# The lists of sources of a graph kernel: 17 gathers of pieces for three nodes each, moved into place on VectorE, for 49 gathers of a list for one node each

## The chip, the core and the metric

The kernel runs on one core of a Trainium2 chip. The time is device microseconds of a whole execution, the median of the runs. One further execution was recorded by the hardware profiler, and all views shown here are of that one. The engines are called by the names of the profile: PE (TensorE matmul) and PEld (its weight loads), DVE (VectorE), ACT (ScalarE), POOL (GpSimd), SP (SyncE, here only a queue of DMAs). "L998" is line 998 of the kernel.

## The reference, cut to what matters

The input is a table `x` of 6250 nodes with 256 features and 100000 edges `src`, `dst`, sorted by `dst`, so that the sources of all edges into one node stand in one run of `src`.

```
x = layernorm(x + two_gatv2_layers(x, edges and a loop at each node))   # 4 heads of 64
x = layernorm(x + gat_layer(x, edges))                                  # 8 heads of 32

xl, xr = x @ Wl, x @ Wr                                  # of each gatv2 layer
logit  = sum over a head of att * leaky_relu(xl[src] + xr[dst])
alpha  = softmax of logit over the edges of one dst
out    = sum over the edges of one dst of alpha * xl[src]  + b
```

## The kernel before, in words

The kernel has two parts, one after the other: `make_plan`, and `tile_by_degree`, which runs the three layers. A third part, `tile_general_path`, runs instead of the layers if the plan finds that its assumptions do not hold (the flag `fits`).

**The layers.** The nodes are put in order of their degree and taken 128 at a time, in NB = 49 blocks. In one block each partition holds one node, and all nodes have about the same number of edges. For each block POOL issues one indirect DMA for each rank of edge (`gather_rows`, L1235): 128 rows of the table, one to a partition. What a node needs for that, the list of its sources (CM = 38 numbers, filled up with the number of an empty row) and its row of `x`, lies in the DRAM table `near_d`, one row to a node in the order of their numbers, and is fetched by `start1` (L1595) with an indirect DMA by `node_i`, the node at each place of the order. The first three fetches come ahead of all gathers of the first layer.

**The plan.** `make_plan` has to deliver four things: `node_i`; the lists in `near_d`; the first layer's table `xl1_d` (x times a weight matrix, 49 blocks of 128 rows, `tables(n)` does the next n blocks); and the place of each node in the order, written beside its row of that table (`place_f`, L1058, 4 bytes to a row). It runs by an order written out by hand; each engine takes its instructions in that order, and so does the queue of each engine that issues DMAs.

1. DVE finds the ends of the runs in `dst` (`ends`, `part`), makes one-hot matrices `oh_lo`, `oh_hi` of the node's two digits, and PE adds up `count`, a [128, 49] table of degrees. A node n is at partition n mod 128 and column n div 128.
2. From `count` come the places at which the lists begin (`begin_i`): PE adds whole columns and the partitions above, DVE sums them up.
3. POOL gathers, for each of the 49 columns, 38 numbers of `list_d` (a copy of `src` in DRAM) from `begin_i` on: one indirect DMA for 128 nodes, 152 bytes each (L998), into `near`.
4. Meanwhile DVE and PE find the order of degrees: one-hot keys `oh`, running sums `cum` by matmuls `pk` in blocks of 512 (`cuts`), `place_f`, the one-hot `to_hi`, `given`, `to_lo`, and the matmuls `pp` that give `node_i`.
5. `lacking` marks which of the 38 numbers are beyond a node's degree, `fill` replaces them (a copy under a mask, L1013) and sends nine columns to `near_d` by a DMA on SP (L1016). The six groups of nine columns (`spans`) are filled where the order by hand puts them: two after step 4, and the others between the tables that are left.
6. DVE adds up what must not be (`wrong`, `bad`), PE sums it over the partitions (`pb`), and `fits` results. `right` and `left` make the weights of the second layer.
7. Between these steps stand `tables(12)`, `(1)`, `(2)`, `(12)`, `(4)`, `(7)` and the remaining 11. One block is: PE turns x (`pt`), ACT copies it (`xT`), PE multiplies (`pm`), ACT copies the row (`xl`, ten buffers), SP sends it to `xl1_d` (L846). SP also loads x (L815) and sends it on to `near_d` (L821), each for seven blocks, and loads the weights `wh` (L1122) and four small rows `fixed` (L1129, L1133) for the later layers.

When the plan ends, its buffers are given to the layers. The first instruction of POOL in the layers (`numbers`, L1182) waits for every DMA and engine that used them.

## Time and profile before

| | us |
|---|---|
| median of 3 runs | 3889.89 (3889.52 to 3891.73) |
| the profiled execution, whole time | 3880.55 |
| its span, first to last instruction | 3878.7 |
| POOL's first gather of lists (L998) begins | 40.07 |
| its last one (of 49) begins | 113.31 |
| last list filled on DVE (L1013) begins | 115.88 |
| POOL's first instruction in the layers (L1182) | 149.98 |
| `start1` of the first block (L1595) | 150.75 |

In the timeline a line is: start, duration, engine, line, operation, output and inputs, how many, and in brackets how long the engine stood idle just before and what ended that. A DMA's instruction on POOL ends when it is issued, not when the data have landed; "SPq" is SP's queue, again the issue. "issue" in brackets is time in which the profile shows nothing that was waited for, and "remote" a release by something it cannot name. Page rows of a group give busy time, mean duration of one in ns, and the idle time before.

### The profile page before, as it was taken

To read this page: it belongs to the slowest core of one execution; us is meant where nothing else is said; L and a number is where in the kernel's file an instruction comes from. 1 tells how busy PE (TensorE), PEld (TensorE's weight loads), DVE (VectorE), ACT (ScalarE), POOL (GpSimd) and SP (SyncE) were. 2 spreads that over 40 slices of the span, in tenths; PEclk is the share of its full clock that TensorE was granted. 3 is DMA by queue.
4 is the path that set the end of the run, shared out by engine and by line. 5 is a ranking of instruction groups with operands and counts; after the bars stand their busy time and mean duration, and the time that the engine had idled before them with its cause. 6 is when DMAs were issued, how large, how long until landed. Compare 5 with 4: busy or idle time off the path is not lost.

```text
span 3878.7 us, 23608 instructions
## 1 busy us (share of the span) xinstructions
PE 1481.8 (38%) x5130; PEld 1113.8 (29%) x5130; DVE 2836.2 (73%) x2648; ACT 1091.1 (28%) x4176; POOL 2530.5 (65%) x2613
## 2 busy tenths in 40 slices
PE   6324665556667763355544545554000000000000
PEld 5213444434555542343433433443000000000000
DVE  6228988668888876899876988896676565666665
ACT  3113444334445442243433434443000000000000
POOL 6464666666666645666666666664777777777774
PEclk8656877778788886676666677776555555555555
DMA  8532333333434334333433434442343333333332
GB/s 188 109 92 78 98 104 104 100 99 103 105 102 108 104 79 109 100 106 104 112 107 105 111 107 110 109 111 74 101 108 101 96 97 96 97 97 96 97 97 57
DMA packets 196123, 395.60 MB, mean 102 GB/s; under 512 B 63036, under 2 KB 115514, under 8 KB 195956
## 3 DMA queue, kind: packets, MB, share of 16 engines
q0 software_dynamic: 122048, 338.04, 33.2%
q1 hardware_dynamic: 66226, 54.22, 5.1%
q10 hardware_dynamic: 7698, 1.74, 0.4%
q8 instruction: 45, 0.74, 0.1%
q14 instruction: 106, 0.87, 0.1%
HBM read 353.82 MB, written 40.42 MB: 102 GB/s over the span
## 4 chain that ended last, share of the span: by engine, by line
issue 20%; POOL 20%; DVE 13%; PE 10%; another core or an unknown queue 6%; ACT 5%; DMA 1%; DVEq 0%; POOLq 0%; ACTq 0%
POOL g L1235 18%; PE acc L1418 6%; DVE z L1505 4%; DVE z L1504 4%; DVE lg L1506 3%; PE pm L1362 3%; ACT g L1410 2%; ACT wt L1381 2%; DVE g L1411 1%; POOL out L1733 1%; DMA g<-xl_d,near_r 1%; DVE weighted L1433 1%; ACT xT L1357 0%; PE pt L1355 0%
## 5 line engine op out<-in xcount | busy, mean ns | idle before, releaser
L1235 POOL DMA_INDIRECT g<-xl_d,near_r x1569 | 1487.4, 948 | 858.7 <-issue 454.3
L1418 PE MATMUL acc<-g,ident 128*128 128x256 f32 x3408 | 1015.9, 461 | 765.3 <-issue 282.7
L1418 PEld LDWEIGHTS acc<-g,ident 128*128 128x128 f32 x3408 | 774.4, 234 | 1004.2 <-issue 522.3
L1235 POOL DMA_INDIRECT g<-whs_d,near_r x766 | 793.2, 1036 | 284.2 <-issue 250.0
L1410 ACT ACTIVATE g<-g,by 128x64 f32<-128x64 f32 x2056 | 545.1, 337 | 316.1 <-issue 310.8
L1504 DVE TENSOR_TENSOR z<-g,pr 128x1820 f32<-128x1820 f32 (+4 forms) x234 | 497.1, 2125 | 19.1 <-DMA g<-xl_d,near_r 10.0
L1505 DVE TENSOR_TENSOR z<-z,at 128x1820 f32<-128x1820 f32 (+4 forms) x234 | 497.4, 2126 | 8.0
L1506 DVE TENSOR_REDUCE lg<-z 128x28 f32<-128x1820 f32 (+4 forms) x234 | 497.3, 2125 | 8.1
L1442 DVE TENSOR_REDUCE acc_v<-weighted 128x256 f32<-128x4096 f32 (+15 forms) x49 | 343.7, 7014 | 16.5 <-remote 8.3
L1411 DVE TENSOR_TENSOR g<-g,wt 128x1792 f32<-128x1792 f32 (+8 forms) x234 | 348.4, 1505 | 2.9
L1391 ACT ACTIVATE wt<-lg 128x128 f32<-128x128 f32 (+17 forms) x49 | 14.0, 285 | 851.0 <-DVE top L1374 391.5
L1703 DVE TENSOR_TENSOR lg<-g,s_r 128x56 f32<-128x56 f32 (+4 forms) x111 | 22.1, 213 | 315.1 <-DMA g<-whs_d,near_r 272.5
L1357 ACT COPY xT<-pt 128x256 f32<-128x256 f32 x147 | 54.9, 374 | 688.5 <-remote 342.2
L1433 DVE TENSOR_TENSOR weighted<-g,wt 128x1792 f32<-128x1792 f32 (+4 forms) x111 | 226.6, 2056 | 0.1
L1571 DVE RECIPROCAL den<-den 128x4 f32<-128x4 f32 x98 | 17.4, 177 | 212.9 <-ACT wt L1381 165.2
L1381 ACT ACTIVATE wt<-lg,top 128x19 f32<-128x19 f32 (+14 forms) x392 | 116.0, 296 | 190.8 <-DVE lg L1506 74.3
L1362 PE MATMUL pm<-wcat,xT 128*128 128x260 f32 x392 | 136.0, 505 | 56.3 <-ACT xT L1357 49.8
L1362 PE MATMUL pm<-wh_cat,xT 128*128 128x272 f32 x196 | 77.5, 531 | 183.8 <-ACT xT L1357 95.5
L1537 DVE TENSOR_TENSOR h<-acc,den 128x256 f32<-128x256 f32 x98 | 40.7, 416 | 126.2 <-remote 112.8
L1362 PEld LDWEIGHTS pm<-wcat,xT 128*128 128x128 f32 x392 | 94.8, 255 | 90.5 <-ACT xT L1357 64.6
L1362 PEld LDWEIGHTS pm<-wh_cat,xT 128*128 128x128 f32 x196 | 42.8, 242 | 203.0 <-ACT xT L1357 104.7
L1362 PE MATMUL pl<-wcat,xT 128*128 128x260 f32 x196 | 64.0, 455 | 55.5 <-issue 40.4
(232 smaller groups left out, 1548.4 us busy)
## 6 DMA issues: line engine op xcount, KB each, us to landing
g<-xl_d,near_r POOLq DMA_INDIRECT x1569
g<-whs_d,near_r POOLq DMA_INDIRECT x766
whs_d<-row SPq DMA_DIRECT2D x49, 132.0 KB
xl_d<-xl SPq DMA_DIRECT2D x49, 130.0 KB
xl_d<-row SPq DMA_DIRECT2D x49, 130.0 KB
xr_d<-row SPq DMA_DIRECT2D x49, 130.0 KB
two<-xl_d SPq DMA_DIRECT2D x49, 130.0 KB
two<-xr_d SPq DMA_DIRECT2D x49, 130.0 KB
```

The costliest lines, as they stand in the source:

```text
L1235: nc.gpsimd.indirect_dma_start(out=g[:, j + own - s0, :width], out_offset=None, in_=table, in_offset=source(of, b, j),)
L1357: nc.scalar.copy(xT, pt)
L1362: nc.tensor.matmul(pm, xT[:, c, :], w[:, c, :], start=c == 0, stop=c == 1)
L1381: nc.scalar.activation(wt[:, :, h], lg[:, :S, h], AF.Exp, bias=top[:, h : h + 1], accum_out=den[:, h : h + 1],)
L1410: nc.scalar.mul(g4[:, t, h, :], g4[:, t, h, :], by[:, t - m, h : h + 1])
L1411: nc.vector.tensor_mul(g4[:, :m], g4[:, :m], wt[:, s0 : s0 + m, :].unsqueeze(3).to_broadcast([P, m, H, F // H]),)
L1418: nc.tensor.matmul(acc, ident, g4[:, t], start=s0 + t == 0, stop=s0 + t == S - 1 and not more)
L1433: nc.vector.tensor_mul(prod[:, s0 - base : s1 - base, :].rearrange("p t (h d) -> p t h d", h=H), g[:, :n, :F].rearrange("p t (h d) -> p t ...
L1442: nc.vector.reduce_sum(part, prod[:, : s1 - base, :].rearrange("p s f -> p f s"), axis=AX.X)
L1504: nc.vector.tensor_max(z, g[:, :n, :W2], xr[:, None, :].to_broadcast([P, n, W2]))
L1505: nc.vector.tensor_mul(z, z, at[:, None, :].to_broadcast([P, n, W2]))
L1506: nc.vector.reduce_sum(lg[:, s0:s1, :], z.rearrange("p t (h d) -> p t h d", h=H2), axis=AX.X)
```

## The change

The number of a node is cut another way: node n is at partition n div 49 and column n mod 49, so that the nodes of one partition are neighbours, and so are their runs in `src`. Division by 49 is a product with `by` and a shift by `down`. One gather now fetches a piece of 133 numbers (532 bytes) for three neighbouring nodes of each partition, from 32 places ahead of the first one's begin; 17 gathers (`SEGS`) cover the 49 columns. `usual` is where each of the three would begin at 16 edges a node; `off` is the deviation from that, cut to 0 to 63 as `off_i`, and its six bits are masks. DVE moves the pieces by powers of two: for each of the three nodes a copy of 69 numbers and a copy under the mask of bit 5 from 32 further on, then for bits 4 to 0 copies under masks within `moved`. A deviation beyond 0 to 63 makes `wrong`.

This stands behind `to_lo` and `pp`, followed by all six `lacking` and `fill`, and only then by `got`, `wrong` and `fits`. The tables are dealt out anew: 12, 1, then one each inside the two loops over `cuts` ahead of the third block and one between the loops, 12, 8 (ahead of `off`), 4, 2 and 7. The four loads of `fixed` come after the last table.

```diff
+    by, down = next(
+        (m, d) for d in range(24, 8, -1) for m in (-(-(1 << d) // NB),)
+        if (NP - 1) * m < 1 << 24 and all(n * m >> d == n // NB for n in range(NP))
+    )
+    assert NP * by >> down >= P
+
+
+    SEGS, STEP, BITS = 17, 3, 6
+    LEAD = 1 << BITS - 1
+    MEAN = E // N
+    LONG = MEAN * (STEP - 1) + CM + 2 * LEAD - 1
+    WIDE = CM + LEAD - 1
+    assert (SEGS - 1) * STEP < NB <= SEGS * STEP
...
-    list_d = dram.tile([-(-E // CM) * CM + CM], I32, name="list_d")
+    list_d = dram.tile([-(-(LEAD + E) // LONG) * LONG + LONG], I32, name="list_d")
...
+    nc.scalar.dma_start(list_d[:LEAD].unsqueeze(0), nothing[:, :LEAD])
+    nc.scalar.dma_start(list_d[LEAD + E :].unsqueeze(0), nothing)
     nc.scalar.dma_start(
-        list_d[:E].rearrange("(a b) -> a b", a=a), src.rearrange("(a b) -> a b", a=a)
+        list_d[LEAD : LEAD + E].rearrange("(a b) -> a b", a=a), src.rearrange("(a b) -> a b", a=a)
     )
...
+    usual = iota("usual", [P, SEGS * STEP], [[0, SEGS], [MEAN, STEP]], base=-LEAD)
...
-    nc.vector.tensor_scalar(
-        part[:, 0, :], run_i, SHIFT, P - 1, op0=OP.logical_shift_right, op1=OP.bitwise_and
+    nc.vector.tensor_single_scalar(part[:, 1, :], run_i, SHIFT, op=OP.logical_shift_right)
+    nc.vector.tensor_single_scalar(part[:, 0, :], part[:, 1, :], float(by), op=OP.mult)
+    nc.vector.tensor_single_scalar(part[:, 0, :], part[:, 0, :], down, op=OP.logical_shift_right)
+    nc.vector.scalar_tensor_tensor(
+        part[:, 1, :], part[:, 0, :], -float(NB), part[:, 1, :], op0=OP.mult, op1=OP.add
     )
-    nc.vector.tensor_single_scalar(part[:, 1, :], run_i, SHIFT + 7, op=OP.logical_shift_right)
...
-    pc = ps.tile([P, 2, NB], F32, name="pc", tag="ph")
-    nc.tensor.matmul(pc[:, 0, :], ones, count, start=True, stop=True)
-    nc.tensor.matmul(pc[:, 1, :], above, count, start=True, stop=True)
+    total = one.tile([P, 1], F32, name="total")
+    nc.vector.reduce_sum(total, count, axis=AX.X)
+    pc = ps.tile([P, 2], F32, name="pc", tag="ph")
+    nc.tensor.matmul(pc[:, 1:], above, total, start=True, stop=True)
+    nc.tensor.matmul(pc[:, :1], ones, total, start=True, stop=True)
+    upto = one.tile([P, NB], F32, name="upto")
+    nc.vector.tensor_tensor_scan(upto, ones_k[:, :NB], count, 0.0, op0=OP.mult, op1=OP.add)
+    within = one.tile([P, SEGS, STEP], F32, name="within")
+    flat = within.rearrange("p s j -> p (s j)")
+    nc.vector.memset(flat[:, NB - 1 :], 0.0)
+    nc.vector.tensor_sub(flat[:, :NB], upto, count)
+    base = one.tile([P, 2], F32, name="base")
+    nc.vector.tensor_copy(base, pc)
+    begin_f = one.tile([P, SEGS], F32, name="begin_f")
+    nc.vector.tensor_scalar(begin_f, within[:, :, 0], base[:, 1:], None, op0=OP.add)
+    begin_i = one.tile([P, SEGS], I32, name="begin_i")
+    nc.vector.tensor_scalar(begin_i, begin_f, float(E), 0.0, op0=OP.min, op1=OP.max)
+    piece_of = one.tile([P, SEGS, LONG], I32, name="piece_of")
+    listed = list_d.rearrange("(a b) -> a b", b=LONG)
+    for k in range(SEGS):
+        nc.gpsimd.indirect_dma_start(
+            out=piece_of[:, k, :], out_offset=None, in_=listed,
+            in_offset=bass.IndirectOffsetOnAxis(ap=begin_i[:, k : k + 1], axis=1),
+        )
     key = one.tile([P, NB], BF16, name="key_b")
     nc.vector.tensor_scalar(key, count, float(high), float(low), op0=OP.min, op1=OP.max)
     nc.vector.tensor_scalar(key, key, -1.0, float(high), op0=OP.mult, op1=OP.add)
...
-    block = one.tile([P, NB], F32, name="block")
-    nc.vector.tensor_copy(block, pc[:, 0, :])
-    upto = one.tile([P, NB], F32, name="upto")
-    nc.vector.tensor_tensor_scan(upto, ones_k[:, :NB], block, 0.0, op0=OP.mult, op1=OP.add)
-    from_f = one.tile([P, NB], F32, name="from_f")
-    nc.vector.tensor_sub(from_f, upto, block)
-    nc.vector.tensor_add(from_f, from_f, pc[:, 1, :])
-    begin_i = one.tile([P, NB], I32, name="begin_i")
-    nc.vector.tensor_scalar(begin_i, from_f, float(E), 0.0, op0=OP.min, op1=OP.max)
-    near = one.tile([P, NB, CM], I32, name="near")
-    no = one.tile([P, NB, CM], I32, name="no")
-    listed = list_d.rearrange("(a b) -> a b", b=CM)
-    for k in range(NB):
-        nc.gpsimd.indirect_dma_start(
-            out=near[:, k, :], out_offset=None, in_=listed,
-            in_offset=bass.IndirectOffsetOnAxis(ap=begin_i[:, k : k + 1], axis=1),
-        )
...
-    spans = [(k, min(NB, k + 9)) for k in range(0, NB, 9)]
-
-    def lacking(k0, k1):
-        shape = [P, k1 - k0, CM]
-        nc.vector.tensor_tensor(
-            no[:, k0:k1, :], ranks[:, None, :].to_broadcast(shape),
-            count[:, k0:k1].unsqueeze(2).to_broadcast(shape), op=OP.is_ge,
-        )
-
-    def fill(k0, k1):
-        shape = [P, k1 - k0, CM]
-        nc.vector.copy_predicated(
-            near[:, k0:k1, :], no[:, k0:k1, :], far[:, None, :].to_broadcast(shape)
-        )
-        nc.sync.dma_start(
-            near_d[k0 * P : k1 * P, :CM].rearrange("(k p) c -> p k c", p=P).bitcast(I32),
-            near[:, k0:k1, :],
-        )
-
-
-    tables(1)
     oh = one.tile([P, KEYS, NB], BF16, name="oh")
     nc.vector.tensor_tensor(
         oh, steps, key[:, None, :].to_broadcast([P, KEYS, NB]), op=OP.is_equal
     )
+
+
+    tables(1)
...
     for c0, c1 in cuts:
+        if c0 == 2 * 512:
+            tables(1)
         pk = ps.tile([P, 512], F32, name="pk", bufs=2)
         nc.tensor.matmul(pk[:, : c1 - c0], ones_b, ohf[:, c0:c1], start=True, stop=True)
         nc.vector.tensor_tensor_scan(
             cum[:, c0:c1], ones_k[:, : c1 - c0], pk[:, : c1 - c0],
             cum[:, c0 - 1 : c0] if c0 else 0.0, op0=OP.mult, op1=OP.add,
         )
-    tables(2)
+    tables(1)
     for c0, c1 in cuts:
+        if c0 == 2 * 512:
+            tables(1)
         pk = ps.tile([P, 512], F32, name="pk", bufs=2)
         nc.tensor.matmul(pk[:, : c1 - c0], less, ohf[:, c0:c1], start=True, stop=True)
         nc.vector.tensor_add(cum[:, c0:c1], cum[:, c0:c1], pk[:, : c1 - c0])
...
-            xl1_d[:NP, W2:].rearrange("(b p) w -> p b w", p=P), place_f.unsqueeze(2)
+            xl1_d[:NP, W2:].rearrange("(p b) w -> p b w", b=NB), place_f.unsqueeze(2)
...
+    tables(8)
+    off = one.tile([P, SEGS, STEP], F32, name="off")
+    nc.vector.tensor_sub(off, within, usual.rearrange("p (s j) -> p s j", s=SEGS))
+    nc.vector.tensor_sub(off, off, within[:, :, :1].to_broadcast([P, SEGS, STEP]))
+    off_i = one.tile([P, SEGS, STEP], I32, name="off_i")
+    nc.vector.tensor_scalar(off_i, off, 0.0, float(2 * LEAD - 1), op0=OP.max, op1=OP.min)
+    bit = one.tile([P, BITS, SEGS, STEP], I32, name="bit")
+    for k in range(BITS):
+        nc.vector.tensor_scalar(
+            bit[:, k], off_i, k, 1, op0=OP.logical_shift_right, op1=OP.bitwise_and
+        )
+    moved = one.tile([P, SEGS, STEP, WIDE], I32, name="moved")
+    for k in range(STEP):
+        for first_at in (0, LEAD):
+            data = piece_of[:, :, MEAN * k + first_at : MEAN * k + first_at + WIDE]
+            if first_at == 0:
+                nc.vector.tensor_copy(moved[:, :, k, :], data)
+            else:
+                nc.vector.copy_predicated(
+                    moved[:, :, k, :],
+                    bit[:, BITS - 1, :, k : k + 1].to_broadcast([P, SEGS, WIDE]), data,
+                )
+    every = moved.rearrange("p s j w -> p (s j) w")
+    bits = bit.rearrange("p b s j -> p b (s j)")
+    for k in range(BITS - 2, -1, -1):
+        n = CM + (1 << k) - 1
+        nc.vector.copy_predicated(
+            every[:, :, :n], bits[:, k, :].unsqueeze(2).to_broadcast([P, SEGS * STEP, n]),
+            every[:, :, 1 << k : (1 << k) + n],
+        )
+    near = every[:, :NB, :CM]
+    no = one.tile([P, NB, CM], I32, name="no")
+    spans = [(k, min(NB, k + 9)) for k in range(0, NB, 9)]
+    def lacking(k0, k1):
+        shape = [P, k1 - k0, CM]
+        nc.vector.tensor_tensor(
+            no[:, k0:k1, :], ranks[:, None, :].to_broadcast(shape),
+            count[:, k0:k1].unsqueeze(2).to_broadcast(shape), op=OP.is_ge,
+        )
+    def fill(k0, k1):
+        shape = [P, k1 - k0, CM]
+        nc.vector.copy_predicated(
+            near[:, k0:k1, :], no[:, k0:k1, :], far[:, None, :].to_broadcast(shape)
+        )
+        nc.sync.dma_start(
+            near_d.rearrange("(p k) c -> p k c", k=NB)[:, k0:k1, :CM].bitcast(I32),
+            near[:, k0:k1, :],
+        )
     for k in spans:
         lacking(*k)
-    fill(*spans[0])
-    fill(*spans[1])
+        fill(*k)
+    tables(4)
     got = one.tile([P, 3, NB], F32, name="got")
     nc.vector.tensor_copy(got, pp)
     nc.vector.scalar_tensor_tensor(
-        node_i, got[:, 1, :], float(P), got[:, 0, :], op0=OP.mult, op1=OP.add
+        node_i, got[:, 0, :], float(NB), got[:, 1, :], op0=OP.mult, op1=OP.add
...
+    nc.vector.tensor_tensor(
+        wrong[:, KE + NB : KE + 2 * NB], off.rearrange("p s j -> p (s j)")[:, :NB],
+        off_i.rearrange("p s j -> p (s j)")[:, :NB], op=OP.not_equal,
+    )
+    nc.vector.tensor_mul(
+        wrong[:, KE + NB : KE + 2 * NB], wrong[:, KE + NB : KE + 2 * NB], count
+    )
     nc.vector.tensor_scalar(
-        wrong[:, KE + NB :], upto[:, NB - 1 :], float(E), None, op0=OP.not_equal
+        wrong[:, KE + 2 * NB :], base[:, :1], float(E), None, op0=OP.not_equal
...
-    tables(4)
+    tables(2)
...
-    fill(*spans[2])
...
-    fill(*spans[3])
...
-    for k in spans[4:]:
-        fill(*k)
```

## Prediction, made before the changed kernel ran

> **What bounds the kernel now.** I read the page first, then the stretch before the layers in the timeline, engine by engine, then its busy time by windows and its waits. The page's rows:
>
> ```profile
> PE 1481.8 (38%) x5130; PEld 1113.8 (29%) x5130; DVE 2836.2 (73%) x2648; ACT 1091.1 (28%) x4176; POOL 2530.5 (65%) x2613
> ...
> L1235 POOL DMA_INDIRECT g<-xl_d,near_r x1569 | 1487.4, 948 | 858.7 <-issue 454.3
> ```
>
> No engine is full. Once the layers run, POOL issues row gathers most of the time, one each 1.25 us (0.95 and 0.30 of issue). The diff leaves these layers alone; it changes what comes ahead of their first gather. The chain of waits starts at 972 us here, so the head has to be read from the timeline. POOL's, cut:
>
> ```profile
> 40.07 1.36 POOL L998 DMA_INDIRECT near<-list_d,begin_i  x1 [17.38 <-DVE begin_i L993]
> ...
> 56.21 2.46 POOL L998 DMA_INDIRECT near<-list_d,begin_i  x1 [0.30 <-issue]
> ...
> 64.12 6.29 POOL L998 DMA_INDIRECT near<-list_d,begin_i  x1 [0.30 <-issue]
> 70.72 0.97 POOL L998 DMA_INDIRECT near<-list_d,begin_i  x1 [0.30 <-issue]
> ...
> 113.31 0.94 POOL L998 DMA_INDIRECT near<-list_d,begin_i  x1 [0.30 <-issue]
> 149.98 0.24 POOL L1182 IOTA numbers<- 128x128 f32 x1 [35.72 <-DMA near_d<-near]
> ```
>
> The 49 gathers of source lists take POOL from 40.07 to 114.25. Then it stands for 35.7 us, until the last list has landed in `near_d`; start1 follows at 150.75 and the layers run from there. The end of that wait is what this change can move, and nothing works beside it: in the windows view DVE is empty from 120 to 150 us.
>
> ```profile
> 82.00:120.00 38.00, 11.63 (x31) 7.79 (x30) 7.14 (x29) 6.75 (x30) 24.64 (x26) 0.52 0.62 101
> 120.00:150.00 30.00, 15.28 (x80) 12.62 (x78) 0.00 (x0) 8.97 (x28) 0.02 (x1) 0.78 0.88 160
> ```
>
> (columns: PE, PEld, DVE, ACT, POOL busy; clock; DMA share; GB/s). Why the lists are that late is on the SP queue and behind it:
>
> ```profile
> 81.57 0.58 DVE L1013 COPY_PREDICATED near<-no,far 128x342 int32<-128x342 int32 x1 [9.16 <-DMA near<-list_d,begin_i]
> ...
> 115.88 0.33 DVE L1013 COPY_PREDICATED near<-no,far 128x152 int32<-128x152 int32 x1 [4.16 <-DMA near<-list_d,begin_i]
> ```
> ```profile
> 141.91 1.35 SPq L1016 DMA_DIRECT2D near_d<-near  x2
> ```
> ```profile
> 110.33 0.38 ACT L845 COPY xl<-pm 128x260 f32<-128x260 f32 x1 [10.14 <-remote]
> 116.61 0.37 ACT L836 COPY xT<-pt 128x256 f32<-128x256 f32 x1 [5.91 <-remote]
> ```
>
> The last list is filled on DVE at 116, but SP issues it at 142.9, behind the rows of the last tables. Those are late because PE and ACT nearly stood from 91 to 117 (PE's clock 0.52), in waits that the trace cannot name; from 119 a table takes 1.1 us again. So two things hold the start: the gathers to 116, and a tail of tables and row writes.
>
> **The change part by part.** Order on the queues, by the diff.
>
> *Before the gathers.* Two more TENSOR_SCALARs on `part` (0.11 apart): +0.25. The ones matmuls become single-column, `block` and two adds give way to total, within, base, begin_f: about even, and the keys now come after begin_i. Gathers start near 40. The first-pass and second-pass loops each get a table ahead of their third block: one table at the low clock is about 1.5 us on DVE's chain (a table was 2.1 us at 42 to 46). So to_hi starts near 54.5 instead of 52.4 and to_lo ends near 71.5 instead of 69.6.
>
> *17 gathers for 49.* 128 rows each as before, so about 0.94 + 0.30: the first ends at 41.4, and by 54.5 some 12 are issued. The rest meet to_hi, three given and to_lo. In the trace one gather ends 0.8 to 0.9 us after each of these (6.29 us at 64.12 under to_lo, 62.91 to 69.59). Five gathers, five instructions: the last ends at 71.5 + 0.9 = 72.4. The Trainium skill, "SBUF — State Buffer", "SBUF: two separate sides", says that a DVE operation with two SBUF inputs takes the shared port from a GpSimd operation that reads SBUF, and a gather reads its indices there. The trace grants that for the bf16 rows above and not in general: `cum`*`oh` (two SBUF inputs, 1.28 us from 48.12) left the gather at 49.23 at 0.99, and `no` left the one at 70.72 at 0.97. By the rule in full, up to three more of the first 12 gathers slip behind the bf16 rows, and POOL ends 3 x 1.25 = 3.8 us later; I take the rows, zero, and keep 3.8 for the range.
>
> *Landing.* place_f's 6272 writes of 4 bytes (L1058, issued 66.16; the new order of rows leaves their number) fill the DMA engines in about 70 to 81. In the trace the second list, whose last gather ended at 74.43, could be filled only at 81.57: 7 us. Idle, 2 us are usual (113.31 + 0.94 to 115.88: 1.6). So the pieces land between 74.5 and 79.5. I take 78, as it is the same storm. Off and the six bits, nine operations of 49 to 51 elements (about 0.2 each, 1.5 us), lie in that wait.
>
> *The moves, all on DVE in series.* The copy with mask has two rows: 342 elements 0.545, 152 elements 0.331; so 0.16 + 1.126 ns an element.
> - three first copies under mask of 17 x 69 = 1173: 1.48 each, 4.4
> - five under mask of 51 x (53, 45, 41, 39, 38) = 11016 elements: 12.4 + 5 x 0.16 = 13.2
> - three plain copies of 1173: the nearest 1-element row gives 1.48 each, 4.4 in all. The Trainium skill, "VectorE: DVE Perf Modes", "What auto-detection actually checks", has a one-source copy in SBUF run two elements a cycle if the outermost dimensions are equal (17 and 17); the TENSOR_SCALAR row (256 elements, 0.276) shows that speed here, and gives 0.75 each, 2.25. I take 2.25; the other end costs 2.2 us.
> Sum 19.9, with hand-overs 20.5. No row has a mask broadcast along its run and a source shifted in its own tile, so the masked price is open: not below the full-rate 1.04 ns (-1.3 us); above, see the rival.
>
> *Then* six lacking and fill pairs: 5 x (0.41 + 0.545) + 0.53 = 5.3, with gaps 5.9 (the L1006 part ran at 69.5 before, beside waiting gathers). Ends 78 + 20.5 + 5.9 = 104.4, with the last near_d issue close behind: 38 us earlier than 142.9. Their landing (six times 1152 rows of 152 bytes) lies beside what follows.
>
> *What stands behind DVE now.* got, node_i, wrong, bad: 2.8 as from 82.04, plus two small ones: 107.6; pb, many, fits 1.6: 109.2. Formerly fits came at 88.4, so the whole tail behind it is 21 us later than it was. On PE, pb stands ahead of the last 7 tables (turned blocks are ready); on ACT left(1) does. left(1): prods at 110.2, eight accumulations of 0.25, ends 112.4. 7 tables: 1.1 each, two of them at 2.1 with the clock down: 10, so 122.4. These 7 were not bounded by fits before but by the standstill, 91 to 122.
>
> *SP.* Rows 37 on wait behind the six near_d issues in queue order; xl has ten buffers, so 28 to 42 go through on PE and ACT with rows up to 36 already issued. Past 104.4 SP has 13 rows at 0.4, two near_d<-xt, two wh loads; this fits before 122.8. The four fixed loads have moved to its very end: 2.4 us (125.64 to 128.1 before), 125.2, and their landing is now waited for: 3 to 6.7 us (142.89 to 149.98 before, with 768 KB ahead). I take 4. POOL's iota at 129, start1 at 129.8.
>
> **Sum.** 150.75 - 129.8 = 21 us earlier. Nothing in the layers takes it back that I can find: their gathers, tiles and counts are the same, and what they wait for first is start1. The nodes of equal degree come in another order, which changes rows, not numbers of them. Against the profiled 3880.55 (span 3878.7 and 1.9 around it): 3859.5. The median of the runs is 3889.89, 9.3 above that execution, so 3869.
>
> **The rivals.**
> *The standstill comes back.* If PE, ACT and SP stand in 91 to 122 whoever gathers, or stand for as long behind fits, the last 7 tables take up to 31 us instead of 10 and the gain is gone (3889); half of it leaves 10 us (3880). For: similar unnamed waits recur in the layers (the page's chain has 6% under an unknown queue). Against: it ended with the last gather's landing (116), and 13 tables then ran at 1.1 each; here gathers end at 72.
> *Slower: the masked moves.* Place: the eight L1114 and L1122 copies, 17.6 us at my price. All behind them on DVE, fits and the tables' tail is in series, so each us counts. At 2.2 times the price (2.5 ns an element) the 21 us are used up: 3890; from there it is slower, and at three times, 3904. For: no such shape in the trace. Against: both sizes of the row lie on one line near one element a cycle.
> *More gained.* The pieces land at 74.5, the fixed loads in 3 us, the masked copies at full rate: 6 us more, 3863; with the layers falling luckier, 3858.
> *It does not do what it says.* If a node's begin is over 32 places from where 16 edges a node put it, the plan is refused and the general path runs instead of the layers by degree. I counted the deviations over the reference's inputs: -16 to +25. Excluded.
>
> **How the numbers follow.** My forecast (gain 12 to 28 us) 0.62; more gained 0.08; the standstill in part (gain 4 to 12, about 3881) 0.13, in full (3889) 0.06; slower by the moves or by another stall in the layers 0.11. 0.2% is 7.8 us, about what a measurement can tell from no change, so under 3882.1 is faster: 0.62 + 0.08 + half the partial standstill is near 0.77; same 0.11; slower (over 3897.7) 0.12. The range: below 3857 I leave 0.05; above, the partial standstill is inside and the full one and the slower case out: 3886.
>
> **What would show it.** Right: 17 gathers, the last ending near 72; L1112's first copy near 78; eight masked copies at 1.48 to 3.2 us; last near_d<-moved near 105; fits near 109; POOL's L1246 iota near 129, waiting on a fixed load; DVE not empty before. Wrong: masked copies of 51 x 53 at over 6 us; PE or ACT standing over 10 us after 112; the iota at 129 but the span not shorter by 21, which would mean that the layers, not their start, set the end.

## The result: 18.5 us faster here, 15.7 us slower in a later group of runs, and the profile after

The changed kernel took 3870.99 us (median of 6 runs, 3867.91 to 3878.75), the kernel before beside it 3889.49 us (6 runs, 3885.55 to 3891.73). The ratio is 0.9956, 95% interval 0.9944 to 0.9969. The execution that was profiled took 3867.91 us with a span of 3866.1; that of before took 3880.55, so the two profiles differ by 12.6 us and not by the 18.5 us of the medians.

The page's busy row of after and its largest group, then the two windows ahead of the layers (PE, PEld, DVE, ACT, POOL busy; clock; DMA share; GB/s):

```profile
PE 1467.6 (38%) x5129; PEld 1101.9 (29%) x5130; DVE 2859.8 (74%) x2674; ACT 1096.0 (28%) x4176; POOL 2506.4 (65%) x2582
...
L1299 POOL DMA_INDIRECT g<-xl_d,near_r x1569 | 1488.8, 949 | 853.0 <-issue 459.2
```
```profile
82.00:120.00 38.00, 15.80 (x77) 12.52 (x76) 31.33 (x49) 10.44 (x43) 0.00 (x0) 0.73 0.75 93
120.00:150.00 30.00, 11.23 (x37) 7.76 (x35) 2.91 (x15) 3.85 (x12) 9.96 (x13) 0.61 0.82 174
```

The layers are the same work: the row gathers are still 1569 at 949 ns. In the first window POOL is empty (24.64 us before) and DVE is busy for 31.33 us (7.14 before): that is the change. In the second, POOL has begun on the layers. The timeline of POOL shows where its wait now ends:

```profile
40.38 1.14 POOL L1016 DMA_INDIRECT piece_of<-list_d,begin_i  x1 [17.09 <-DVE key_b L1021]
...
65.10 6.30 POOL L1016 DMA_INDIRECT piece_of<-list_d,begin_i  x1 [0.30 <-issue]
...
72.95 0.95 POOL L1016 DMA_INDIRECT piece_of<-list_d,begin_i  x1 [0.30 <-issue]
122.49 0.24 POOL L1246 IOTA numbers<- 128x128 f32 x1 [48.59 <-DMA near_d<-moved]
...
133.13 0.97 POOL L1659 DMA_INDIRECT near_r<-near_d,node_i  x1 [10.16 <-DMA near_d<-xt]
...
141.43 0.94 POOL L1299 DMA_INDIRECT g<-xl_d,near_r  x1 [4.83 <-DVE few_n L1310]
```

The first row gather of the layers begins at 141.43 us; in the profile of before L1235 begins at 154.53. That is 13.1 us earlier, and the span is 12.6 us shorter: from the first row gather to the end it is 3724.2 us before (3878.7 - 154.5) and 3724.7 after (3866.1 - 141.4). In these two profiles the layers gave nothing and took nothing; the start set the difference. How DVE and SyncE spent the head:

```profile
83.41 0.81 DVE L1112 COPY moved<-piece_of 128x1173 int32<-128x1173 int32 x1 [11.31 <-DMA piece_of<-list_d,begin_i]
84.26 1.54 DVE L1114 COPY_PREDICATED moved<-bit,piece_of 128x1173 int32<-128x1173 int32 x1
...
90.34 13.97 DVE L1122 COPY_PREDICATED moved<-bit,moved 128x2703 int32<-128x2703 int32 x5
...
114.00 0.15 DVE L1184 TENSOR_SCALAR fits<-many 128x1 int32<-128x1 f32 x1
...
140.80 0.17 DVE L1307 CAST few_got<-near_r 128x11 f32<-128x11 int32 x1 [24.72 <-DMA fixed_r<-in_L_gnn_a]
```
```profile
105.33 8.47 SPq L1142 DMA_DIRECT2D near_d<-moved  x6
...
122.35 3.32 SPq L1189 DMA_DIRECT2D wh_cat<-in_L_gnn_W  x2
...
127.70 0.44 SPq L835 DMA_DIRECT2D near_d<-xt  x1
...
133.35 1.08 SPq L1199 DMA_DIRECT2D fixed_r<-in_L_gnn_a  x2
```

ScalarE and TensorE, which stood for 10 to 14 us at a time in before, have no wait without a name behind 78 us: ScalarE's `xl` copies come every 1.1 us from 77.5 to 88.5. ScalarE's long wait after that is `[19.87 <-DVE prod L797]`, so it is VectorE's moves that it waits for.

### The profile page after: what moved, and what is told of

Its sections match the earlier page's. It is cut to its first block, busy times and chain, and to the rows that moved or that the text cites. A ratio compares the mean times of both kernels' runs of the same rounds, so it can differ in the third digit from the quotient of the medians.

```text
span 3866.1 us, 23566 instructions
## 1 busy us (share of the span) xinstructions
PE 1467.6 (38%) x5129; PEld 1101.9 (29%) x5130; DVE 2859.8 (74%) x2674; ACT 1096.0 (28%) x4176; POOL 2506.4 (65%) x2582
## 4 chain that ended last, share of the span: by engine, by line
issue 25%; POOL 23%; DVE 16%; PE 15%; another core or an unknown queue 8%; ACT 7%; DMA 2%; DVEq 0%; ACTq 0%; POOLq 0%
POOL g L1299 21%; PE acc L1482 11%; DVE z L1568 5%; DVE z L1569 4%; DVE lg L1570 3%; ACT g L1474 3%; PE pm L1426 3%; ACT wt L1445 2%; DMA g<-xl_d,near_r 1%; DVE g L1475 1%; POOL out L1797 1%; PE pt L1419 1%; DVE weighted L1497 1%; ACT xT L1421 1%
## 5 line engine op out<-in xcount | busy, mean ns | idle before, releaser
L1445 ACT ACTIVATE wt<-lg,top 128x19 f32<-128x19 f32 (+14 forms) x392 | 116.0, 296 | 189.8 <-issue 69.0
L1426 PE MATMUL pm<-wcat,xT 128*128 128x260 f32 x392 | 123.5, 468 | 48.2 <-issue 26.2
L1426 PEld LDWEIGHTS pm<-wcat,xT 128*128 128x128 f32 x392 | 86.7, 233 | 78.3 <-ACT xT L1421 34.5
```

Of the source, the lines that this page charges most:

```text
L1426: nc.tensor.matmul(pm, xT[:, c, :], w[:, c, :], start=c == 0, stop=c == 1)
L1445: nc.scalar.activation(wt[:, :, h], lg[:, :S, h], AF.Exp, bias=top[:, h : h + 1], accum_out=den[:, h : h + 1],)
```

## The experiments

The runs came in four groups, and each was compared with the kernel before in its own group. The groups differ a good deal: the median of before was 3371.69 us in the first, 3886.03 in the second, 3870.14 in the third and 3373.57 (one run) in the last. So the first and the last are of one sort (below: the 3372 sort), and the others are like the first measurement. The recorded texts speak of chips of two sorts, but that is not shown: the groups are noted as chips 15, 13, 15 and 13, so that each of the two numbers stands once with 3372 and once with 3870 or more; whether one number is one and the same chip is not on record. What the traces show is mostly waiting, not slower work: the changed kernel keeps VectorE busy for 2858.6 us of a span of 3385.1 in the first group, and for 2859.8 of 3866.1 in the first measurement. In the 3372 sort no trace has a wait for "remote"; in the others every trace has some, and the chain of waits gives up to 10% to "another core or an unknown queue".

How far a start of the layers is passed on can be read inside a group, as the time from the first row gather to the end of the profiled execution. In the first group it is 3239.4, 3239.7, 3239.6 and 3241.6 us (the changed kernel and its three variants); in the second 3730.2 for before and 3729.3 and 3727.8 for two variants; in the third 3705.9 for before and 3698.9 and 3712.7. So a start is passed on within some 2 us in the first two groups, and only within about 14 in the third.

**The change again, where the kernel before takes 3371.69 us.** No edit.

> The changed kernel once more, as the neighbour on the same chip for the other three. Theory (the gain is the earlier start of the layers, one for one): 3871 +- 4, some 15 to 19 us under the kernel before. Rival (the layers' own waits moved by chance and made part of the difference): the difference to the kernel before comes out at other than 13 to 19 us here.

A miss: 3387.39 us, ratio 1.0045 (1.0031 to 1.0059). Here the change *loses* 15.7 us. Its head is hardly different from that of the first profile:

```profile
125.81 0.24 POOL L1246 IOTA numbers<- 128x128 f32 x1 [52.52 <-DMA near_d<-moved]
...
145.73 0.94 POOL L1299 DMA_INDIRECT g<-xl_d,near_r  x1 [5.20 <-DVE few_n L1310]
```

So the changed kernel starts its layers at about the same time in both, and what turned the comparison must be the start of the kernel before, or its layers.

**The storm of small writes, moved.** In the same group. ScalarE's write of `place_f` goes from ahead of the turned blocks to behind `tables(8)`:

```diff
-    with nc.allow_non_contiguous_dma(reason="one number to a row"):
-        nc.scalar.dma_start(xl1_d[:NP, W2:]..., place_f.unsqueeze(2))
...
     tables(8)
+    with nc.allow_non_contiguous_dma(reason="one number to a row"):
+        nc.scalar.dma_start(xl1_d[:NP, W2:]..., place_f.unsqueeze(2))
```

> Only the write of place_f (6272 times 4 bytes) is moved on ACT's queue, from ahead of the 8 tables to behind them. Theory (these small writes hold up the landing of the last pieces): DVE's first copy of moved starts at 75 to 77 instead of 83.4, fits 6 to 8 us earlier, and the first row gather up to as much; the small writes then lie at 95 to 107 beside the moves, and may cost the near_d writes some of it: 3864 to 3869. Rival (pieces of 532 bytes land late by themselves): the first copy stays within 2 us of 83.4 and the time at 3871.

```profile
77.28 0.81 DVE L1112 COPY moved<-piece_of 128x1173 int32<-128x1173 int32 x1 [6.95 <-DMA piece_of<-list_d,begin_i]
```

The pieces can be read 6.3 us earlier than in the unedited kernel of this group (77.28 for 83.54), the first row gather comes 6.5 us earlier (139.23 for 145.73), and the time falls by 5.6 us to 3381.75 (ratio 1.0031, 1.0020 to 1.0042). The landing of the pieces behind 6272 writes of 4 bytes is a real cost, and what is saved there comes through to the end, nearly whole.

**The fixed loads, moved.** The two `wh` loads and the four `fixed` loads go right behind `tables(8)`.

> One part undone: the two loads of wh and the four of fixed stand ahead of the six near_d writes on SP, in a stretch in which SP is empty (92.5 to 105.3), not in and behind the last tables. Theory: the layers' first row gather (141.4 in the changed kernel) waited for the landing of the last fixed load, issued at 134.4, and the xl copy at 126.2 waited 4.7 us behind the wh loads; without both the last row is sent near 127 and landed near 130, the first gather comes near 133 to 135: 6 to 8 us less, about 3864. Rival (it is the near_d rows and the last xl rows that everything waits for anyway): first gather at 139 or later, at most 2 us less.

The first row gather comes at 139.17, not at 133 to 135, but that forecast was counted from 141.4; against the 145.73 of this group it is 6.6 us earlier, where 6 to 8 had been expected. The time is 3381.50 (ratio 1.0030, 1.0018 to 1.0041), 5.9 us less. `few_got` no longer waits for the fixed rows; `start1` still waits for features, at 134.91.

**All tables and the loads early.** As the one before, with all remaining 21 tables at the place of `tables(8)`.

> All 21 last tables stand ahead of the moves, and the loads of wh and fixed ahead of the near_d writes; nothing but pb, right and left stands behind fits. Theory (start of the layers sets the time one for one; the tail behind fits is what is left of it): the near_d writes are the last DMAs of the plan, issued by 114 and landed by 118 to 121, first row gather at 121 to 126 instead of 141.4: 15 to 20 us less, about 3854. Rival (the layers give an earlier start back, in waits of their own): first gather as said, but less than 8 us gained in time.

A miss: the first row gather comes at 138.38, not at 121 to 126, and the time is 3381.24 us (ratio 1.0026, 1.0016 to 1.0037). SyncE's queue and POOL show why:

```profile
111.67 13.10 SPq L1156 DMA_DIRECT2D near_d<-moved  x6
```
```profile
133.90 0.24 POOL L1243 IOTA numbers<- 128x128 f32 x1 [61.13 <-DMA near_d<-moved]
```

The rows are all out at 104.7 us, but the six list writes take 13.1 us to issue and have landed only at 133.9. What had to come last was no longer the tail of tables but the lists. The trace keeps a record of every packet. Of the 6272 packets of 152 bytes, the first thousand take 14 ns each on average, the second 23, and each later thousand 65 to 78 ns, from 116.0 to 131.6 us in all; from 118 to 124 us there is next to nothing else among the packets. In the changed kernel's first profile it is 14 and 15 ns, then 43 to 73, from 106.2 to 119.2 us. These averages come from a part of the packets: in that profile 29% of those behind the first thousand take over 25 ns, the others about 14. In the three profiles of before, whose writes go out one or two at a time, the averages by the thousand are 13 to 61 ns.

**Why the list writes are slow.** Two edits of the write, in the group with before at 3886.03. First, the lists go to the rows where the kernel before put them:

```diff
-            near_d.rearrange("(p k) c -> p k c", k=NB)[:, k0:k1, :CM].bitcast(I32),
+            near_d[k0 * P : k1 * P, :CM].rearrange("(k p) c -> p k c", p=P).bitcast(I32),
```

> The changed kernel, with one edit: the six writes of the finished lists go to the rows where the kernel before put them (neighbouring partitions on neighbouring rows of near_d) instead of 49 rows apart, so that the lists stand at other nodes' rows and the output is not the reference's; the work is the same. Theory: the spread of the rows makes the 6272 packets of 152 bytes slow (57 to 78 ns each in the changed kernel, 13 to 44 ns in the kernel before); here they take under 45 ns, the iota of the layers, which waits for these writes, comes at 112 to 117 us instead of 122.5 to 125.8, and the first row gather some 5 us earlier, if fixed loads and features don't take over. Rival: it is the burst, six writes at once over the same 16 engines: packets as slow as before the edit, the iota within 2 us of 122.5 to 125.8, and no change of the time over 2 us against the changed kernel's ratio 1.0045.

Once the burst is under way the packets take 64 to 79 ns on average, and the iota comes at 126.1: no better. (The whole time, 13,699.8 us, holds the general path as well, which ran after layers whose lists did not belong to their nodes.) Second, every sixth node column to a write, `near[:, j::6, :]` for `near[:, k0:k1, :]`:

> The changed kernel, with one edit: each of the six fills and writes takes every sixth node of a partition instead of nine neighbouring ones, so that no two rows of a write are neighbours. Same bytes and packets. If neighbouring rows inside a partition's packet group are what makes the writes slow, packets fall below 50 ns and the iota comes 5 us or more earlier; if the burst or the distance between partitions does, the iota stays within 2 us of the changed kernel's 122.5 to 125.8, and the time within 0.1% of the changed kernel's ratio. I expect the latter.

Packets of 68 to 73 ns on average under way, iota at 125.4, 3876.68 us (ratio 0.9980, 0.9966 to 0.9994). The order of the rows is not the cause; the burst, many small packets at once, is what remains, though no run took it alone away. The first packets of each burst, at 13 to 14 ns, show that the write itself is not slow.

**The kernel before, for its trace, twice.** Unchanged, in the second group and in the third.

> The kernel before, unchanged, for its trace. On the chip of the last runs the changed kernel lost 15.7 us (3387.39 against 3371.69 us) although its first row gather began at 145.73 us, close to where it began in the first profile. Theory: the long stretch of before's first profile in which SyncE, ScalarE and TensorE hardly moved (91 to 117 us) belongs to that execution and not to the program; here it is absent, the first row gather begins at 128 to 133 us instead of 154.53, and the span is about 3369. Rival 1: the stretch is there again (first row gather at 150 or later) and the changed kernel loses its time inside the layers; then the row gathers of the two kernels must differ by some 10 us or more behind 160 us. Rival 2: half of each, first row gather at 136 to 145.

> The kernel before, unchanged, for its trace on this chip. If its median here is near 3885, the stretch in which ScalarE and TensorE stand (92 to 117 us) is there a third time and the first row gather comes at 152 to 160 us. If it is near 3372, the theory says that the stretch is absent and the first row gather comes at 128 to 133 us, 13 to 17 us ahead of the changed kernel's 145.7; the rival says that it comes at 150 or later and that the changed kernel's loss there is in the layers.

The stretch is there both times: the first row gather comes at 158.7 and 161.9 us, so the theory that it belonged to one execution falls. Neither group was of the 3372 sort. From the third group, one line each from the timelines of DVE and PE:

```profile
106.01 0.16 DVE L1114 TENSOR_SCALAR many<-pb 128x1 f32<-128x1 f32 x1 [23.54 <-remote]
```
```profile
115.13 2.10 PE L843 MATMUL pm<-wcat,xT 128*128 128x260 f32 x4 [21.50 <-remote]
```

The product that `many` waits for, `pb`, ran at 82.53 us; VectorE reads it 23 us later. TensorE's records have updates of the semaphore in question at 86.4, 90.6 and 106.0, and VectorE moves with the last one. POOL meanwhile issues its gathers evenly, one each 1.25 us, up to 114.9.

**Gathers added to the changed kernel.** Is it the gathers that let the others stand?

```diff
+    idle = one.tile([P, 32, CM], I32, name="idle")
+    for k in range(32):
+        nc.gpsimd.indirect_dma_start(
+            out=idle[:, k, :], out_offset=None, in_=listed,
+            in_offset=bass.IndirectOffsetOnAxis(ap=begin_i[:, k // 2 : k // 2 + 1], axis=1),
+        )
```

> The changed kernel with 32 gathers more behind its 17, of 38 numbers each as the kernel before gathered them, into a tile that nothing reads: POOL then issues 49 gathers as before, up to about 115 us instead of 74. Nothing else is moved. Theory: it is the gathers that let the other engines stand in the kernel before (ScalarE and TensorE idle 10 to 14 us at a time between 90 and 117 us, SyncE at some 0.7 us an instruction), and the change gains on such a chip by ending them early. Then here, on a chip whose median of before is near 3885, the tables behind the matmuls of the places come as slowly as there, ScalarE and TensorE idle by 10 us or more at once before 117 us, and the first row gather comes at 150 to 160 us; ratio 0.998 to 1.003. Rival 1: what stood was the long fills on VectorE with their writes in between, not the gathers; then the tables are through at about 95 us as in the changed kernel and the first row gather comes at 141 to 146, ratio 0.995 to 0.998. On a chip with before near 3372, by the theory no engine stands, and the ratio is 1.004 to 1.007 for the copies and list writes alone.

3856.48 us, ratio 0.9971 (0.9953 to 0.9989), first row gather at 149.0. The start lies between the two forecasts and the ratio in the second one's range; the lines that decide speak against the theory.

```profile
112.40 0.95 POOL L1022 DMA_INDIRECT idle<-list_d,begin_i  x1 [0.30 <-issue]
113.65 0.95 POOL L1022 DMA_INDIRECT idle<-list_d,begin_i  x1 [0.30 <-issue]
114.91 0.94 POOL L1022 DMA_INDIRECT idle<-list_d,begin_i  x1 [0.31 <-issue]
116.15 0.95 POOL L1022 DMA_INDIRECT idle<-list_d,begin_i  x1 [0.30 <-issue]
```
```profile
116.24 0.16 DVE L1188 TENSOR_SCALAR many<-pb 128x1 f32<-128x1 f32 x1 [0.68 <-PE pb L1186]
```

The same step, `many` behind `pb`, takes 0.68 us here with POOL gathering at full pace beside it, against 23.54 us in the kernel before in the same group. No wait of PE or ACT between 82 and 140 us is put down to "remote", though one of 10.54 us on ACT ends just before, at 78.30. So gathers under way are not enough to make the others stand. The test is not a full copy of the kernel before: between 79 and 108 us, while the tables ran and then the moves, the added gathers mostly came more slowly than one each 1.25 us, and only from 112 us on at that pace. The later start than in the changed kernel comes from POOL itself, which is through with the 49th gather only at 131.1, and comes to its iota, after 4.7 us more for a row of the tables, at 135.8. Even so it is 12.9 us ahead of the 161.88 of the kernel before in this group: most of the gain stays when the gathers are put back.

**The changed kernel in halves.** Towards a better version: tables and loads early, `place_f` late, and the moves in two halves (`for s0, s1 in ((0, 9), (9, SEGS))`), each filled and written before the next.

> The changed kernel with four edits: the remaining tables directly behind the matmuls for the places, the loads of w3 and of the fixed rows behind them, ScalarE's write of the places after those tables, and the move of the lists done in two halves (27 and 24 node columns), each half filled and written before the next is moved. The first three without the halves gave a first row gather at 138.38 us with the lists landing at 133.9. Theory: lists written in one burst at the end are what is late there. With halves the first three writes start about 10 us earlier (near 95 us) and drain while the second half is moved; the last lands at 118 to 124, the first row gather at 126 to 131, and the time 7 to 12 us below that run's 1.0026, which is level with the kernel before (0.998 to 1.001). Rival: the writes are slow for their number, not their start, and with them SyncE: the last lands at 130 or later and the time stays at 1.002 or above.

3869.69 us, ratio 0.9952 (0.9936 to 0.9968), first row gather at 142.92, where 126 to 131 had been expected. SyncE's queue:

```profile
103.50 8.32 SPq L1100 DMA_DIRECT2D fixed_r<-in_L_gnn_b  x2
111.87 3.38 SPq L1104 DMA_DIRECT2D fixed_r<-in_L_gnn_a  x2
116.66 13.17 SPq L1140 DMA_DIRECT2D near_d<-moved  x6
```

The first three lists were ready at 85.2 us, ten earlier than expected, and the last three at 98.4. But in SyncE's order all six stood behind the last rows and the fixed loads, and these beside the 4-byte writes, whose packets now ran from 101 to 115; so the halves went out together, in one burst from 116.66 on. (The next expectation repeats the 95 us; it is 85.2.) Then the order was changed: `place_f` after three tables, the first list writes after 14, loads behind the last table.

> The version in halves with another order of queues: ScalarE's write of the places after three of the 21 tables (about 80 us) instead of behind all, 11 tables, the first half of the moves with its three list writes, 7 tables, the loads of w3 and the fixed rows, the second half. In the earlier version SyncE's queue held the first list writes, ready at about 95 us, until 116.7 us, behind fixed loads that took 11.7 us to issue while 6272 packets of 4 bytes from the write of the places filled the 16 engines (1.84 of them busy at a time by overlapping records). Theory: that order was what cost; here the first three list writes go out at 92 to 97 us, the last lands at 116 to 122, the first row gather comes at 124 to 132, and the time falls by 10 to 18 us below the earlier version: ratio 0.990 to 0.993 on a chip with before near 3885, 0.996 to 1.000 on one near 3372. Rival: the fixed loads or the attention's work behind the lists end last again; first row gather at 136 or later, ratio within 0.002 of the earlier version's 0.9952.

3855.93 us, ratio 0.9966 (0.9948 to 0.9984), against an expected 0.990 to 0.993: missed again. The first row gather is at 140.29. The intervals of these two and of the change (0.9956) overlap; neither is shown to be better than the change.

```profile
100.77 4.59 SPq L1127 DMA_DIRECT2D near_d<-moved  x3
...
123.59 4.43 SPq L1127 DMA_DIRECT2D near_d<-moved  x3
```

The last list was filled at 98.2 us, yet its write was issued near 128: seven rows and six loads stand ahead of it on SyncE. The rows were late because ScalarE waited 6.8 us for an `xl` buffer, held by the 4-byte writes at 78 to 86. Each version moved the same queueing to another place.

**The kernel before with 17 of its 49 gathers.** The one trace of before's order in a group of the 3372 sort.

```diff
-    for k in range(NB):
+    nc.gpsimd.memset(near[:, 17:, :], 0)
+    for k in range(17):
```

> The kernel before with 17 of its 49 list gathers; the lists of the other 32 node columns are set to zero by one POOL memset ahead of them, so that most lists are not the graph's: only the time up to the first row gather is to be read, not the whole time. Everything else keeps its place in every queue. Theory: the stretch in which ScalarE and TensorE stand (83 to 117 us in three profiles of before) needs gathers under way on POOL behind 82 us. POOL is then through with them at about 62 us; the tables and ScalarE's sums run through without a wait of 5 us or more that no tile explains, and the first row gather comes at 122 to 134 us instead of 154.5 to 161.9. Rival: the stretch comes from the order of the work (loads and list writes between the tables on SyncE's queue, the small sums for the test); then it is there again, and the first row gather comes at 145 or later. On a chip with before near 3372 both give 120 to 134, and nothing is told apart.

```profile
129.57 0.24 POOL L1183 IOTA numbers<- 128x128 f32 x1 [55.83 <-DMA near_d<-near]
...
134.12 0.94 POOL L1236 DMA_INDIRECT g<-xl_d,near_r  x1 [0.30 <-issue]
```

On the question of the standing it tells nothing apart, as the expectation said. It does show that 32 gathers fewer, with nothing else moved, leave a wait of 55.83 us for the lists, whose last writes SyncE issues at 120.6 to 122.6, behind the tail of tables. So in this sort it is that tail, and not the gathers, that holds the start here; with all 49 gathers the last list would be filled at 116 to 118 us, if that comes as in the three traces of before, and that too is ahead of 120.6. (Most of its lists are zeros, so that its 3611.51 us is no measure.)

## Why the prediction was right, and where its steps were off

The predicted 3869.0 us is 2 us from the measured 3870.99. The reason given for it, that the wait in front of the layers ends earlier and the layers pass that on, is what the two profiles show. But the forecast of 21 us consists of terms of which several were wrong, and that the number fits to 2 us is luck.

- *Gathers.* Right: 40.38 for "near 40", one gather held by each bf16 operation, the last one ending at 73.90 for 72.4. One gather more was held, by `cum`*`oh`, for about 1 us of the 3.8 us kept in the range: the zero there was wrong (below).
- *Landing.* Mis-sized: 83.41 for 78. The pieces kept VectorE waiting for 11.31 us beside the storm of 4-byte writes; in the first group 6.3 us of that wait went when the write was moved.
- *Moves.* Right: 83.41 to 104.3 is 20.9 us, for 20.5. Plain copies took 0.79 to 0.81 us, which is the two elements a cycle that the skill's rule gave (0.75), not 1.48. Copies under mask took 1.53 to 1.55 us (1.48), the five long ones 13.97 (13.2). The rival that saw these as the danger, and needed 2.2 times the price, did not occur.
- *List writes "beside what follows".* Wrong. The last was to be issued near 105; they took 8.47 us to issue, until 113.80, and their landing held POOL until 122.49. (They are five writes of 1152 rows and one of 512, not six of 1152.) In this profile that was covered by the next term, but once the tables were moved away (138.38 us, above) it was the bound.
- *SyncE's tail.* Mis-sized: 13 rows at 0.4 us were to be through by 122.8. Six rows took 6.34 us, the last six 4.09, and the last one was out at 132.33.
- *The last landing.* The step that named the fixed loads as what POOL's iota and `start1` wait for failed. The iota, forecast near 129, came at 122.49 behind the lists; `start1` waits for the last features, `near_d<-xt`, issued at 127.70, and begins at 133.13 for 129.8. The fixed rows come later still, and hold `few_got` until 140.80. The time from `start1` to the first row gather, 3.8 us in before and taken as unchanged, became 8.3.

The zero came from a wrong reading of the trace. The prediction took the rule of the Trainium skill ("SBUF — State Buffer", "SBUF: two separate sides") as not granted for `cum`*`oh`, since in the first profile of before the gather beside that operation took only 0.99 us:

```profile
48.12 1.28 DVE L1044 TENSOR_TENSOR cum<-cum,oh 128x1078 f32<-128x1078 f32 x1
```
```profile
49.23 0.99 POOL L998 DMA_INDIRECT near<-list_d,begin_i  x1 [0.31 <-issue]
```

But the operation ended at 49.40, only 0.17 us after this gather had begun. Where more of it was left, the gather was held, in the changed kernel until 0.82 us behind its end, and in the third profile of the kernel before for 1.87 us:

```profile
49.17 1.28 DVE L1051 TENSOR_TENSOR cum<-cum,oh 128x1078 f32<-128x1078 f32 x1
```
```profile
49.35 1.92 POOL L1016 DMA_INDIRECT piece_of<-list_d,begin_i  x1 [0.30 <-issue]
```

Put together: 21 us, less 3.3 at `start1`, less 4.5 behind it, is the 13.1 us by which the first row gather is earlier (with rounding). The medians give 18.5; the other 5.4 us lie between executions, since the profiled run of before was 8.9 us under its median and that of after 3.1 us. The prediction added 9.3 us to the changed kernel for this, and what that was too much, 6.2 us (9.3 less 3.1), covered most of the 8.3 us of gain that the profiles lack.

The rival of a standstill that comes back did not occur in the first profile: no such wait behind 78 us. But the prediction's reason against it, that the standing ended with the gathers, is not shown to be the cause: with 32 gathers put back beside the changed kernel's work the standing did not return, and the kernel stayed faster than before (ratio 0.9971). So the runs do not show that the fewer gathers are what gains; the other order of the work, which the change brought along, is as open. The standing was seen in all three profiles of before, in groups with before at 3870 to 3890, between about 83 and 117 us; which of fills, loads and writes between the tables takes part was not tried.

That also bears on the loss in the first group. The changed kernel starts its layers there at 145.73 and is 15.7 us slower than before. Moved starts came through nearly whole there (6.6 us for 5.9, 6.5 for 5.6, 7.4 for 6.2). If the layers of before take the 3239.6 us of the others in that group, it started near 130 us, with no standing, and the change only adds its chain on VectorE. The 17-gather kernel's 134.12 and the absence of unnamed waits fit this in the main, but 134.12 is 4 us later although that kernel gathers less. It is argued, not shown: the kernel before was not traced in such a group.

## What to carry to other kernels

A gain that is read from a stretch in which engines stand for reasons the trace does not name belongs to that measurement until another one shows it: here the same change moves the time by -18.5 us in one and by +15.7 us in another. Put back what the change took away, alone, before naming it as the cause: here the gain outlived the gathers. Before moving work out of the way, write down what each in-order queue then holds ahead of the last transfer; of five versions that shifted tables, loads and writes, none was clear of the next item in SyncE's queue. And 6272 small writes at once were DMA work of 8 to 18 us in these traces, to be given a place of their own, not counted as "beside".

## What the runs showed of the hardware that was not expected

- 6272 packets of 152 bytes in one burst began at 14 ns each and went on at 43 to 80 ns on average by the thousand, 13 to 16 us together in the profiles of the changed kernel and its variants of the first group; neighbouring or distant rows made no difference. SyncE, issuing into the burst, needed up to 13.17 us for six writes, and two fixed loads took 8.32 us beside the 4-byte writes (0.92 us in the changed kernel).
- A gather that began while a VectorE operation with two inputs in SBUF was under way ended some 0.8 us behind that operation, whatever the type: bf16 (2.26 to 6.30 us a gather), fp32 with bf16 (up to 1.92), and copies under mask on 32-bit numbers, beside which the added gathers took 1.94 to 3.11 us from 89 to 107 us, and 0.95 from 112 on. An operation that was nearly over cost it next to nothing (0.99).
- The same program ran in 3372 us in two groups of runs and in 3870 to 3889 us in the others, at about the same granted clock (0.69 and 0.66 to 0.67 for the profiled kernels); the changed kernel kept VectorE busy for the same time in both sorts (2858.6 and 2859.8 us), so the difference is mostly waiting.
